# Aggregation of a graph convolution by seven products of 2x2 blocks, with the sums of counts made during the projection

## The chip, the cores and the metric

The kernel runs on one core of a Trainium2 chip. The metric is the device time of one execution in microseconds, as the median of several runs. One further execution was taken with the hardware profiler, and its record is what "the profile" and "the trace" mean here. The engines are TensorE (PE; its weight loads are listed apart as PEld), VectorE (DVE), ScalarE (ACT), GpSimd (POOL) and SyncE (SP). SP only issues DMA transfers; POOL issues some as well.

## The reference

There are 1250 nodes with 1024 features, and 20000 edges. Four parts follow each other, each on a normalized copy of x and added to x: graph attention, a feed-forward layer with a wide projection, a graph convolution, and a layer of eight experts. The change is in the convolution:

```python
x = x + _L0_gnn_ref(_layernorm(x), W, a_l, a_r, src, dst)
x = x + _L0_ffn_ref(_layernorm(x)[None], rail_maker, rail_up_proj, w_cproj)[0]
x = x + _L1_gnn_ref(_layernorm(x), edge_index, W, b)
x = x + _L1_ffn_ref(_layernorm(x)[None], w1s, w2s, w3s, W1, W2, W3, Wg)[0]

def _L1_gnn_ref(x, edge_index, W, b):
    ei = jnp.concatenate([edge_index, jnp.stack([self_idx, self_idx])], axis=1)
    row, col = ei
    h = jnp.einsum('nd,od->no', x, W) + b
    deg = jnp.zeros((num_nodes,)).at[row].add(1.0)
    norm = deg[row] ** -0.5 * deg[col] ** -0.5
    return jax.ops.segment_sum(norm[:, None] * h[col], row, num_segments=num_nodes)
```

Written with matrices, the last line is D (C + I) D h: C counts the edges from each node to each other node, I stands for the edge of each node to itself, and D is the diagonal of deg to the power -0.5.

## The kernel before

The 1250 nodes are ten tiles of 125 (`R` = 125, `T` = 10). While it works on the attention, the kernel builds the counts from the edge list and keeps them in DRAM as `cnt_d[s, p, d, j]`: the number of edges from node j of tile s to node p of tile d. A block of 125x125 counts read this way has the summed index on the partitions, as a matmul's weights need it.

The feed-forward layer comes next and is the longest stage. Its projection multiplies hidden rows with `w_cproj` in 16 blocks. Each block is done as 2x2 blocks by seven products, twice nested: 49 steps in the blocks 0 to 14, and 28 steps in block 15. A step is `product` (four matmuls with 313 columns, L594; the trace has two records for each fp32 matmul), and then `accumulate`: ACT copies the result out of PSUM to one of five buffers `parts` (L603), and a DMA from POOL's queue adds it onto `acc_d` in DRAM (L605 for block 0, L607 for the rest). The sums of blocks of weights and of hidden rows, which the seven products take as factors, are made on DVE by `add_up` (L587) some steps ahead of their use; `projection_plan` lists the steps and decides ahead of which one each sum stands. Hidden rows lie in buffers `YS` of 128 x 626 numbers, which are views into the tiles `X` and `low`. The free ones are the list `yh`, taken by `place_y`, and given back by `used` after their last reader. SP loads the weights (L406, `load_weights`) and the rails of the next block (`load_rails`, L413 and L414). The loop over the steps (L703) holds the order in which all this is issued; in it `b` is the block and `m` the step in the block. A scheduler places the instructions on each engine by this order, and an engine runs its own in order.

In the last block, `x` and the accumulated sums are read back, and `linear` (L779) then computes h for each tile of nodes: DVE adds the bias (L786), and ACT multiplies the rows with `dis`, the diagonal D. The result is `Hs`, ten tiles of 125 x 1024, which takes the memory of `low`.

The aggregation (L847 to L866) goes over the ten row tiles r. For each it has the counts of that row in one of three slots of the tile `first_w`, loaded by `load_counts` three rows ahead (SP's queue; POOL adds the identity to the diagonal block, L795). It makes 20 matmuls: ten column tiles c, two halves g of 512 features, into a PSUM tile `ph` of two banks. DVE multiplies the result with `dis` and adds it into X (L861), normalizes the row (`normalize`, L138 to L145), and SP stores it to `xn_d`. PE turns row r-1 between two rows (`turn`, L153: eight transposes and two copies by ACT), and at r = 5, r = 9 and the end makes the `logits` (L840) that choose the experts. `dma` issues two transfers, for partitions 0 to 111 and 112 to 124 (L105, L106). The layer of experts follows (L885 and after).

The factors of the seven products are the same tables for the projection and for the changed aggregation:

```python
SUMS = {"X": {"s1": ("21", "+", "22"), "s2": ("s1", "-", "11"), "s3": ("11", "-", "21"), "s4": ("12", "-", "s2")},
        "Y": {"s1": ("12", "-", "11"), "s2": ("22", "-", "s1"), "s3": ("22", "-", "12"), "s4": ("s2", "-", "21")}}
FACTORS = {1: ("11", "11"), 2: ("12", "21"), 3: ("s4", "22"), 4: ("22", "s4"), 5: ("s1", "s1"), 6: ("s2", "s2"),
           7: ("s3", "s3")}
```

Of the kernel before, what the change touches and what calls it, by code (L numbers as in the profile page):

```python
# [8 lines left out]
F32 = mybir.dt.float32  # L9
# [5 lines left out]
ALU = mybir.AluOpType  # L15
# [4 lines left out]
P = 128  # L20
R, T = 125, 10
N = R * T
# [12 lines left out]
NS = NE * ROWS // P  # L35
NP = N + 2
NQ = NP // 4
NB = 16


# [2 lines left out]
FACTORS = {1: ("11", "11"), 2: ("12", "21"), 3: ("s4", "22"), 4: ("22", "s4"), 5: ("s1", "s1"), 6: ("s2", "s2"),  # L43
           7: ("s3", "s3")}
# [53 lines left out]
def gnn_ffn_kernel(ctx, tc, x, src, dst, gat_w, a_l, a_r, maker, up, cproj,  # L98
                   gcn_w, gcn_b, w1s, w2s, w3s, w1, w2, w3, wg, out):
    nc = tc.nc  # L100
    ctx.enter_context(nc.allow_non_contiguous_dma(reason="weights by blocks"))

    def dma(eng, out, in_):

        eng.dma_start(out[:RA], in_[:RA])  # L105
        eng.dma_start(out[RA:], in_[RA:])  # L106
# [7 lines left out]
    nm_d = dram.tile([T, R, N], F32, name="nm_d")  # L114
    x_d = dram.tile([T, R, D], F32, name="x_d")

    acc_d = dram.tile([7, 7, P, 2, NQ], F32, name="acc_d")
    xn_d = dram.tile([N, D], F32, name="xn_d")
    tok_d = dram.tile([NE * ROWS + N, 1], I32, name="tok_d")
# [27 lines left out]
    def turn(xT, norm, psp, t, bufs=2, at=None, wide=False):  # L147

        at = t * R if at is None else at
        for g in range(2):  # L150
            pt = psp.tile([P, 4, 512], F32, name="pz2")[:, :, :R] if wide else psp.tile([P, 4, R], F32, name="pt", bufs=bufs)
            for k in range(4):
                nc.tensor.transpose(pt[:, k, :], norm[t][:, (4 * g + k) * P:(4 * g + k + 1) * P], ident[:R, :R])  # L153
            nc.scalar.copy(xT[:, 4 * g:4 * g + 4, at:at + R], pt)
# [229 lines left out]
    X = XX[:R]  # L384
    for t in range(T):
        dma(nc.gpsimd, X[:, t, :], x_t[t])
    HN = N // 2
    HT = T // 2
    norm = {}
    tt = nc.vector.tensor_tensor  # L390

# [146 lines left out]
    with ExitStack() as tail:  # L538
# [26 lines left out]
        def place_y(top):  # L565

            return yh.pop(yh.index(max(yh)) if top else 0)
# [41 lines left out]
        def late_tile(t):  # L609
            xn = scratch[:R, (4 + t % 2 * 2) * 512:][:, :D]  # L610
            normalize(norm, rlp, t, xn)
            turn(xT, norm, zps, t, 1, t * R + 1, wide=True)


        def free_acc(v):
            (yh if v < 32 else early).append(v)
# [81 lines left out]
        last, j = None, 0  # L698
        loads_at = dict(zip((end + v for v in (-13, -6, 1, 7, 12, 15, 20)), OUTER))
        bring = [(end + v, k, outer_sums(w)) for v, k, w in zip((-9, 0, 3, 10, 14, 18, 22), (2, 2, 2, 4, 4, 3, 3), OUTER)]  # L700
        added, sent = [], []
        norm = {}
        for n, (b, p, i, pairs) in enumerate(steps):  # L703
            m = n - 49 * b
            if n >= end - 70:

                xw[:] = [v for v in xw if v < 33]
            for w in (b, b + 1):
                while coming.get(w) and len(xw) > (0 if w == b else 16 if m < 12 else 8 if m < 20 else 4):
                    load_weights(w, *coming[w].pop(0))  # L710
            if b == 0:
                for v in first.get(m, ()):
                    hidden(0, *v)
            while j < len(sums) and sums[j][0] <= n:
                add_up(*sums[j][1:])
                j += 1
            if b == 0 and m in late:
                late_tile(late[m])
                if late[m] == T - 1:
                    xw += range(33, 41)  # L720
            if b == 0 and m == 30:

                for e in range(NE):
                    nc.gpsimd.dma_start(
                        ys_d[:NE * ROWS, :].rearrange("(p s) (a b) -> p s a b", s=NS, b=128)[CAP - P:, 2 * e + 1],
                        zero[CAP - P:].to_broadcast([ROWS - CAP, D // 128, 128]))
            if b + 1 < NB:
                if m == 20:
                    for k in range(2):
                        load_rails(b + 1, k)  # L730
                if m in (28, 30):
                    rails(m // 2 - 14, zps.tile([P, 4, 512], F32, name="pz2")[:, 0, :P])
                if m in later:
                    hidden(b + 1, *later[m])
            assert n != end - 13 or all(v < 33 for k, v in buf.items() if k[1] == "X")
            if n in loads_at:
                load_sums(loads_at[n])
            if n == end:
                blocks.close()
                tl = rest.enter_context(tc.tile_pool(name="tl", bufs=2))  # L740
                psp = rest.enter_context(tc.tile_pool(name="tps3", bufs=2, space=PSUM))
                yh += parts
            if b == NB - 1:
                if m >= 14 and len(W3) < 2 * KD:
                    for g, k in [(g, k) for g in range(2) for k in range(KD)]:
                        with tc.issue_after(sent[0]):
                            at = [v for v in xw if not 8 <= v < 16]
                            if at and (k, g) not in W3:
                                xw.remove(at[0])
                                W3[k, g] = XS[at[0]].rearrange("p q o -> p (q o)")  # L750
                                nc.gpsimd.dma_start(W3[k, g], gcn_w[k * P:(k + 1) * P, g * 512:(g + 1) * 512])
                if m == 23:
                    nc.gpsimd.dma_start(bias, gcn_b.partition_broadcast(R))
                while m >= 16 and len(fetched) < 4 and fetch(len(fetched)):
                    pass
                if m == 22:
                    add_out(0)
                    level(0)
                if m == 24:
                    turn_tile(0)  # L760
                if m == 27:
                    add_out(1)
                    level(1)
            po = product(pairs)
            if last:
                (combine if last[0] == NB - 1 else accumulate)(*last[last[0] == NB - 1:])
            for n0, k, sums_of in bring:
                if n0 <= n:
                    with tc.issue_after(added[-1]) if n > end else nullcontext():
                        for _ in range(k):  # L770
                            next(sums_of, None)
            last = b, p, i, po
# [13 lines left out]
            tt(Hs[:, t, :], ph.rearrange("p a b -> p (a b)"), bias, op=ALU.add)  # L786
            nc.scalar.activation(Hs[:, t, :], Hs[:, t, :], AF.Copy, scale=dis[:, t:t + 1])

        def counts(r):

            return first_w[:R, r % 3 * N:r % 3 * N + N].rearrange("p (t j) -> p t j", j=R)

        def load_counts(r):
            dma(nc.sync, counts(r), cnt_d[r])
            nc.gpsimd.tensor_tensor(counts(r)[:, r, :], counts(r)[:, r, :], ident[:R, :R], op=ALU.add)  # L795

        for t in range(T):
            if 5 <= t < 8:
                load_counts(t - 5)
            for w in range(len(fetched), min(T, t + 5)):  # L800
                fetch(w)
            linear(t)
# [22 lines left out]
        weights(wsh, w1s, w2s, w3s)  # L825
        wgt = keep.tile([P, KD, NE], F32, name="wgt")
        nc.sync.dma_start(wgt, wg.rearrange("(k p) e -> p k e", p=P))
        hs = keep.tile([P, 2, N], F32, name="hs")
        late = keep.tile([R, T, NE], F32, name="late")
        place = keep.tile([R, T], I32, name="place")  # L830
        back = keep.tile([R, T], I32, name="back")
# [4 lines left out]
        def logits(t0, n):  # L836

            pg = psp.tile([NE, 512], F32, name="pg", bufs=1)
            for k in range(KD):
                nc.tensor.matmul(pg[:, :n * R], wgt[:, k, :], xT5[:, k, t0 * R:(t0 + n) * R],  # L840
                                 start=(k == 0), stop=(k == KD - 1))
            lgT = lnp.tile([NE, 512], F32, name="lgT", bufs=2)
            nc.scalar.copy(lgT[:, :n * R], pg[:, :n * R])
            for i in range(n):
                nc.tensor.transpose(pl[:, t0 + i, :], lgT[:, i * R:(i + 1) * R], ident[:NE, :NE])

        for r in range(T):  # L847
            cs = counts(r)
            pa = psp.tile([R, 2, 512], F32, name="ph")
            for c in range(T):  # L850
                for g in range(2):
                    nc.tensor.matmul(pa[:, g, :], cs[:, c, :], Hs[:, c, g * 512:(g + 1) * 512],  # L852
                                     start=(c == 0), stop=(c == T - 1))
            if r:
                turn(xT5, norm, psp, r - 1)
                if r in (5, 9):
                    logits(r - 5, 4)
            if r + 3 < T:
                load_counts(r + 3)
            xs = X[:, r, :]  # L860
            nc.vector.scalar_tensor_tensor(xs, pa.rearrange("p a b -> p (a b)"), dis[:, r:r + 1], xs,  # L861
                                           op0=ALU.mult, op1=ALU.add)
            normalize(norm, lnp, r)
            dma(nc.sync, xn_d[r * R:(r + 1) * R, :], norm[r])
        turn(xT5, norm, psp, T - 1)
        logits(8, 2)  # L866
        lg = lnp.tile([R, T, NE], F32, name="lg", bufs=1)
        nc.vector.tensor_copy(lg, pl)

# [2 lines left out]


    with back_end:
        with tc.tile_pool(name="ab", bufs=2, space=PSUM) as abp, tc.tile_pool(name="tps", bufs=2, space=PSUM) as tps, \
                tc.tile_pool(name="ops6", bufs=1, space=PSUM) as ops:

# [206 lines left out]
```

## Time and profile before

| | us |
|---|---|
| median of 3 runs | 2962.14 (2961.96 to 2962.9) |
| the profiled execution | 2961.7 |
| its span, first to last instruction | 2959.9 |
| PE busy | 2896.8 (98% of the span) |
| DVE busy | 1593.2 (54%) |
| ACT busy | 875.9 (30%) |
| POOL busy | 764.1 (26%) |
| attention and hidden rows, until | 680 |
| projection, blocks 0 to 14, until | 2317 |
| last block and `linear`, until | 2467 |
| aggregation, until | 2668 |
| experts, until | 2959.9 |

The span is what the profiler recorded; the time of the execution has 1.8 us more around it. A busy share is the time in which an engine has an instruction under way. PE can be busy in the record while its matmuls, which overlap, advance slower or faster, so lengths of stages are read from the starts of instructions. An engine that is not on the chain of waits can be far from full without any loss, and can be delayed without any loss until somebody waits for it.

### The profile page before, as it was taken

The page shows a single profiled execution, that of the slowest core. Times are in us where ns is not written, and L with a number is a line of the kernel's source. Part 1 is how long each engine was busy: PE and PEld are TensorE (multiplying, and loading weights), DVE is VectorE, ACT ScalarE, POOL GpSimd, SP SyncE. Part 2 cuts the span into 40 slices and gives each one's busy share as a digit, 9 for nine tenths or more (in the row PEclk, how much of TensorE's full clock was granted, in tenths as well). Part 3 has the DMA queues.
Part 4 walks back from the last instruction along what each step waited for, and adds up shares of the span by engine and source line. Part 5 has one row for each costly group of instructions (what it writes and reads, how often), then busy time and mean ns, then how long its engine had stood idle before and what let it go on. Part 6 is the DMA issues. An engine that isn't in the chain of part 4 may idle for free.

```text
span 2959.9 us, 32455 instructions
## 1 busy us (share of the span) xinstructions
PE 2896.8 (98%) x11479; PEld 1911.6 (65%) x11479; DVE 1593.2 (54%) x2611; ACT 875.9 (30%) x1415; POOL 764.1 (26%) x982
## 2 busy tenths in 40 slices
PE   8999899999999999999999999999999999999997
PEld 5574677666766766766766766766767544445774
DVE  7687887845645645645645645645467431221113
ACT  1221234444344344344344344344330110000000
POOL 2010000224434434434434434434330000002001
PEclk9999999999999999999999999999999999999999
DMA  5245523569999999999999999999994302222655
GB/s 142 65 114 143 152 70 119 186 162 178 194 168 179 195 167 179 194 168 180 192 168 182 191 167 182 192 164 163 208 245 132 81 0 74 62 70 72 215 196 165
DMA packets 252549, 449.58 MB, mean 152 GB/s; under 512 B 48160, under 2 KB 132218, under 8 KB 251753
## 3 DMA queue, kind: packets, MB, share of 16 engines
q0 software_dynamic: 115216, 270.53, 53.7%
q1 hardware_dynamic: 137162, 176.86, 20.3%
q8 instruction: 96, 1.57, 0.2%
q14 instruction: 75, 0.61, 0.1%
HBM read 175.38 MB, written 271.89 MB: 151 GB/s over the span
## 4 chain that ended last, share of the span: by engine, by line
PE 83%; DVE 1%; DMA 1%; ACT 0%; issue 0%; POOL 0%; DVEq 0%; ACTq 0%
PE po L594 56%; PE ph L852 6%; PE pab L885 6%; PE po L779 5%; PE pz L428 3%; PE po L448 3%; PE po L991 2%; PE po L1002 1%; PE pt L153 1%; DMA low<-acc_d 1%; PE pg L840 1%; DMA yg<-ys_d,back 0%; DMA rowbd<-st 0%; PE px L679 0%; PE pt L981 0%
## 5 line engine op out<-in xcount | busy, mean ns | idle before, releaser
L607 POOL DMA_DIRECT2D acc_d<-low x686 | 592.9, 865 | 915.2 <-ACT low L603 890.3
L603 ACT COPY low<-po 128x626 f32<-128x626 f32 x735 | 501.0, 682 | 994.3 <-PE po L594 822.4
L594 PE MATMUL po<-X,arena 128*128 128x313 f32 x2160 | 608.2, 428 | 0.0
L594 PEld LDWEIGHTS po<-X,arena 128*128 128x128 f32 x2160 | 404.8, 189 | 171.3 <-issue 19.2
L594 PE MATMUL po<-low,arena 128*128 128x313 f32 x1568 | 443.5, 428 | 0.0
L594 PEld LDWEIGHTS po<-low,arena 128*128 128x128 f32 x1568 | 294.0, 189 | 123.2 <-issue 12.4
L594 PE MATMUL po<-X,first_w 128*128 128x313 f32 x856 | 243.3, 428 | 0.2 <-DVE first_w L587 0.2
L594 PE MATMUL po<-X,BZ 128*128 128x313 f32 x720 | 207.1, 431 | 0.0
L594 PEld LDWEIGHTS po<-X,first_w 128*128 128x128 f32 x856 | 160.5, 189 | 68.0 <-issue 7.5
L852 PE MATMUL ph<-low,first_w 125*125 125x512 f32 x400 | 173.6, 593 | 1.4 <-issue 1.4
L594 PEld LDWEIGHTS po<-X,BZ 128*128 128x128 f32 x720 | 135.7, 191 | 57.8 <-issue 7.7
L587 DVE TENSOR_TENSOR X<-X 128x626 f32<-128x626 f32 x141 | 114.3, 813 | 101.3 <-PE po L594 99.8
L594 PE MATMUL po<-low,first_w 128*128 128x313 f32 x544 | 155.3, 429 | 0.0
L209 PE MATMUL pz<-W,xT 128*125 128x512 f32 x320 | 141.2, 596 | 0.1
L594 PE MATMUL po<-low,BZ 128*128 128x313 f32 x480 | 138.4, 428 | 0.0
L852 PEld LDWEIGHTS ph<-low,first_w 125*125 125x125 f32 x400 | 74.3, 188 | 94.8 <-issue 94.8
L594 PEld LDWEIGHTS po<-low,first_w 128*128 128x128 f32 x544 | 101.6, 190 | 43.2 <-issue 5.5
L587 DVE TENSOR_TENSOR X<-low,X 128x626 f32<-128x626 f32 x101 | 82.0, 816 | 84.4 <-PE po L594 82.4
L587 DVE TENSOR_TENSOR low<-X 128x626 f32<-128x626 f32 x102 | 82.8, 815 | 69.3 <-PE po L594 69.1
L587 DVE TENSOR_TENSOR X<-X,low 128x626 f32<-128x626 f32 x92 | 75.1, 818 | 80.3 <-PE po L594 80.1
L277 PE MATMUL pc<-os,od 125*125 125x417 f16 (+1 forms) x588 | 110.9, 345 | 5.1 <-issue 5.1
L448 PE MATMUL po<-BZ,w 125*125 125x257 f32 x400 | 96.6, 401 | 19.5 <-DVE w L446 18.2
(263 smaller groups left out, 3405.5 us busy)
## 6 DMA issues: line engine op xcount, KB each, us to landing
acc_d<-low POOLq DMA_DIRECT2D x735, 313.0 KB, 5.9
arena<-in_cproj SPq DMA_DIRECT2D x148, 256.0 KB
w<-in_w SPq DMA_DIRECT2D x16, 1024.0 KB
BZ<-in_cproj SPq DMA_DIRECT2D x56, 256.0 KB
first_w<-in_cproj SPq DMA_DIRECT2D x52, 256.0 KB
nm<-nm_d SPq DMA_DIRECT2D x20, 546.9 KB
w3t<-in_w SPq DMA_DIRECT2D x8, 1024.0 KB
X<-acc_d SPq DMA_DIRECT2D x20, 313.0 KB
```

Of the source, the lines that this page charges most:

```text
L209: nc.tensor.matmul(pz, xT[:, k, t * R:(t + 1) * R], W[g][:, k], start=(k == 0), stop=(k == KD - 1))
L277: nc.tensor.matmul(pc[:, b, :nn], od[:, d - near[c][0], :], os[:, n0:n0 + nn], start=(c == win[d][0]), stop=(c == win[d][-1]))
L428: nc.tensor.matmul(pz, [*rail_parts(k)][-1][rows, :], xT[rows, (2 * b + k) % KD, n * NQ:(n + 1) * NQ], start=True, stop=True)
L448: nc.tensor.matmul(po[i], w[:, i * R:(i + 1) * R], Z[h // 2][:, s, h % 2, :], start=(s == 0), stop=(s == T - 1))
L587: tt(view(k), *a, op=ALU.add if sign == "+" else ALU.subtract)
L594: nc.tensor.matmul(po[:, o, :NQ], view(x)[:, q, o * P:(o + 1) * P], view(y)[:, q, :], start=(i == q == 0), stop=(i + 1 == len(pairs) and q ...
L603: nc.scalar.copy(part, po[:, :, :NQ])
L607: sent[:] = [nc.gpsimd.dma_start(out=acc_d[p - 1, i - 1], in_=part, accum_op=ALU.add).ins]
L779: nc.tensor.matmul(ph[:, g, :], turned[t][:, k, :], W3[k, g], start=(k == 0), stop=(k == KD - 1))
L852: nc.tensor.matmul(pa[:, g, :], cs[:, c, :], Hs[:, c, g * 512:(g + 1) * 512], start=(c == 0), stop=(c == T - 1))
L885: nc.tensor.matmul(pab[:, :nn], w12[:, i, k, f * P:(f + 1) * P], rhs[:, k, n0:n0 + nn], start=(k == 0), stop=(k == KD - 1))
L991: nc.tensor.matmul(po[:m, g, :], hid[:, f, s * P:s * P + m], w3t[:, f, g * 512:(g + 1) * 512], start=(f == 0), stop=(f == 1))
```

## The change

The aggregation is written as a product of 2x2 blocks, (C + I) by `Hs`. A block of C + I is 5 x 5 tiles of 125; a block of `Hs` is five tiles by 512 features. Seven products with sums of blocks take the place of eight products of blocks.

The sums of counts are made within the projection. In each of the blocks 2 to 6, at step 24, `load_pair` takes four `YS` buffers and loads into them one column tile c and its partner c + 5 of the counts (eight transfers on SP, with runs of 125 numbers, 500 bytes). At step 31 `sum_pair` adds the identity to the two diagonal blocks, makes the four sums s1 to s4 on DVE, stores them to `s_d` in DRAM (eight transfers on SP), and gives the buffers back.

The aggregation is then a list of 35 items (p, a): product p, row tile a of five. An item is five matmuls of 512 columns into one PSUM bank, with four banks in rotation. Its counts, half as wide as before, lie in one of six slots and are loaded six items ahead, from `s_d` or from `cnt_d`. Each result is added on DVE straight into the halves of rows of X which it belongs to (`into`: one to four of them; a new tile `ndis` has the negative of `dis`). The sums of `Hs` are made on DVE, up to three after each item; s1 and s2 have a new tile each, s3 overwrites block 12, and s4 block 21 once product 2 is done. A row is complete with product 3 or 4, and is normalized then; it is turned two items later. The tile `hs` of the experts moves to another pool.

```diff
+    s_d = dram.tile([4, HT, R, HT, R], F32, name="s_d")
...
+        def as_counts(i):
+            return YS[i].rearrange("p q n -> p (q n)")[:R, :HN].rearrange("p (a j) -> p a j", j=R)
+
+        def load_pair(c):
+            pair[:] = [place_y(False) for _ in range(4)]
+            for i, (s0, d) in zip(pair, ((0, c), (HT, c), (0, c + HT), (HT, c + HT))):
+                dma(nc.sync, as_counts(i), cnt_d[s0:s0 + HT, :, d, :].rearrange("s p j -> p s j"))
+
+        def sum_pair(c):
+            x11, x21, x12, x22 = (as_counts(i) for i in pair)
+            for v in (x11, x22):
+                tt(v[:, c, :], v[:, c, :], ident[:R, :R], op=ALU.add)
+            tt(x22, x21, x22, op=ALU.add)
+            tt(x21, x11, x21, op=ALU.subtract)
+            tt(x11, x22, x11, op=ALU.subtract)
+            tt(x12, x12, x11, op=ALU.subtract)
+            for k, v in enumerate((x22, x11, x21, x12)):
+                dma(nc.sync, s_d[k, :, :, c, :].rearrange("a p j -> p a j"), v)
+            yh.extend(pair)
...
+            if 2 <= b < 2 + HT:
+                if m == 24:
+                    load_pair(b - 2)
+                if m == 31:
+                    sum_pair(b - 2)
...
+        work = [(p, a) for p in (1, 2, 6) for a in range(HT)]
+        work += [(p, a) for w in ((5, 3), (7, 4)) for a in range(HT) for p in w]
+
+        def counts(i):
+            return first_w[:R, i % 6 * HN:i % 6 * HN + HN].rearrange("p (c j) -> p c j", j=R)
+
+        def load_counts(i):
+            p, a = work[i]
+            cs = counts(i)
+            f = FACTORS[p][0]
+            if f[0] == "s":
+                dma(nc.sync, cs, s_d[int(f[1]) - 1, a])
+                return
+            d0 = HT * (f[1] == "2")
+            dma(nc.sync, cs, cnt_d[HT * (f[0] == "2") + a][:, d0:d0 + HT, :])
+            if f[0] == f[1]:
+                nc.gpsimd.tensor_tensor(cs[:, a, :], cs[:, a, :], ident[:R, :R], op=ALU.add)
...
-                load_counts(t - 5)
+                load_counts(2 * t - 10)
+                load_counts(2 * t - 9)
...
-        hs = keep.tile([P, 2, N], F32, name="hs")
...
-        for r in range(T):
-            cs = counts(r)
-            pa = psp.tile([R, 2, 512], F32, name="ph")
-            for c in range(T):
-                for g in range(2):
-                    nc.tensor.matmul(pa[:, g, :], cs[:, c, :], Hs[:, c, g * 512:(g + 1) * 512],
-                                     start=(c == 0), stop=(c == T - 1))
-            if r:
-                turn(xT5, norm, psp, r - 1)
-                if r in (5, 9):
-                    logits(r - 5, 4)
-            if r + 3 < T:
-                load_counts(r + 3)
-            xs = X[:, r, :]
-            nc.vector.scalar_tensor_tensor(xs, pa.rearrange("p a b -> p (a b)"), dis[:, r:r + 1], xs,
-                                           op0=ALU.mult, op1=ALU.add)
-            normalize(norm, lnp, r)
-            dma(nc.sync, xn_d[r * R:(r + 1) * R, :], norm[r])
-        turn(xT5, norm, psp, T - 1)
-        logits(8, 2)
+        sp = tail.enter_context(tc.tile_pool(name="tsum", bufs=1))
+        Y = {f"{1 + i}{1 + j}": Hs[:, HT * i:HT * i + HT, j * 512:(j + 1) * 512] for i in range(2) for j in range(2)}
+        Y["s1"], Y["s2"] = (sp.tile([R, HT, 512], F32, name=f"y{i}") for i in range(2))
+        Y["s3"], Y["s4"] = Y["12"], Y["21"]
+
+        def sum_h(k, c):
+            u, sign, v = SUMS["Y"][k]
+            tt(Y[k][:, c], Y[u][:, c], Y[v][:, c], op=ALU.add if sign == "+" else ALU.subtract)
+
+        sums_h = [(k, c) for k in ("s1", "s2", "s3") for c in range(HT)]
+        into = {1: ((0, 0, 1), (0, 1, 1), (1, 0, 1), (1, 1, 1)), 2: ((0, 0, 1),), 3: ((0, 1, 1),), 4: ((1, 0, -1),),
+                5: ((0, 1, 1), (1, 1, 1)), 6: ((0, 1, 1), (1, 0, 1), (1, 1, 1)), 7: ((1, 0, 1), (1, 1, 1))}
...
+        def turn_ready():
+            t = ready.pop(0)[1]
+            turn(xT5, norm, psp, t)
+            if t in (4, 8, 9):
+                logits(*{4: (0, 4), 8: (4, 4), 9: (8, 2)}[t])
+
+        for i, (p, a) in enumerate(work):
+            cs = counts(i)
+            pa = psp.tile([R, 512], F32, name="ph", bufs=4)
+            for c in range(HT):
+                nc.tensor.matmul(pa, cs[:, c, :], Y[FACTORS[p][1]][:, c], start=(c == 0), stop=(c == HT - 1))
+            if i + 6 < len(work):
+                load_counts(i + 6)
+            if ready and ready[0][0] <= i - 2:
+                turn_ready()
+            for h, j, sign in into[p]:
+                r = HT * h + a
+                xs = X[:, r, j * 512:(j + 1) * 512]
+                nc.vector.scalar_tensor_tensor(xs, pa, (dis if sign > 0 else ndis)[:, r:r + 1], xs,
+                                               op0=ALU.mult, op1=ALU.add)
+            if (p, a) == (2, HT - 1):
+                sums_h += [("s4", c) for c in range(HT)]
+            for _ in range(min(3, len(sums_h))):
+                sum_h(*sums_h.pop(0))
+            if p in (3, 4):
+                r = a if p == 3 else HT + a
+                normalize(norm, lnp, r)
+                dma(nc.sync, xn_d[r * R:(r + 1) * R, :], norm[r])
+                ready.append((i, r))
+        while ready:
+            turn_ready()
...
+        hs = back_end.enter_context(tc.tile_pool(name="hsp", bufs=1)).tile([P, 2, N], F32, name="hs")
```

More of the change, by code (lines that the diff above doesn't have):

```diff
@@ L37 @@
 NQ = NP // 4
+HN, HT = N // 2, T // 2
 NB = 16
@@ L386, in gnn_ffn_kernel @@
         dma(nc.gpsimd, X[:, t, :], x_t[t])
-    HN = N // 2
-    HT = T // 2
     norm = {}
@@ L700, in gnn_ffn_kernel @@
         bring = [(end + v, k, outer_sums(w)) for v, k, w in zip((-9, 0, 3, 10, 14, 18, 22), (2, 2, 2, 4, 4, 3, 3), OUTER)]
-        added, sent = [], []
+        added, sent, pair = [], [], []
         norm = {}
@@ L787, in linear @@
             nc.scalar.activation(Hs[:, t, :], Hs[:, t, :], AF.Copy, scale=dis[:, t:t + 1])
[L789 to L795, printed above, removed]
+        work = [(p, a) for p in (1, 2, 6) for a in range(HT)]
[13 more added lines that the diff above has]
+                nc.gpsimd.tensor_tensor(cs[:, a, :], cs[:, a, :], ident[:R, :R], op=ALU.add)
         for t in range(T):
             if 5 <= t < 8:
-                load_counts(t - 5)
+                load_counts(2 * t - 10)
+                load_counts(2 * t - 9)
             for w in range(len(fetched), min(T, t + 5)):
@@ new lines, in gnn_ffn_kernel @@
+        sums_h = [(k, c) for k in ("s1", "s2", "s3") for c in range(HT)]
+        into = {1: ((0, 0, 1), (0, 1, 1), (1, 0, 1), (1, 1, 1)), 2: ((0, 0, 1),), 3: ((0, 1, 1),), 4: ((1, 0, -1),),
+                5: ((0, 1, 1), (1, 1, 1)), 6: ((0, 1, 1), (1, 0, 1), (1, 1, 1)), 7: ((1, 0, 1), (1, 1, 1))}
+        ndis = lnp.tile([R, T], F32, name="ndis", bufs=1)
+        nc.vector.tensor_scalar(ndis, dis, -1.0, None, op0=ALU.mult)
+        ready = []
+        def turn_ready():
[3 more added lines that the diff above has]
+                logits(*{4: (0, 4), 8: (4, 4), 9: (8, 2)}[t])
```

## The prediction

> **What bounds the kernel now.** I read the chain of waits first, then the table of windows by stage, then PE's waits inside the two stages that the diff touches, and last the groups by engine. Part 4 of the page:
>
> ```profile
> PE 83%; DVE 1%; DMA 1%; ACT 0%; issue 0%; POOL 0%; DVEq 0%; ACTq 0%
> PE po L594 56%; PE ph L852 6%; PE pab L885 6%; PE po L779 5%; PE pz L428 3%; PE po L448 3%; PE po L991 2%; PE po L1002 1%; PE pt L153 1%; DMA low<-acc_d 1%; PE pg L840 1%; DMA yg<-ys_d,back 0%; DMA rowbd<-st 0%; PE px L679 0%; PE pt L981 0%
> ```
>
> TensorE sets the end, and the two touched places, the projection (L594) and the aggregation (L852), are both on the chain. The windows of these stages (length, busy time and count of PE, PEld, DVE, ACT, POOL, then clock, DMA share, GB/s):
>
> ```profile
> 680.00:2317.00 1637.00, 1636.82 (x6745) 1127.36 (x6744) 937.64 (x1317) 603.81 (x922) 623.28 (x735) 1.00 1.02 180
> 2467.00:2668.00 201.00, 199.66 (x538) 88.48 (x538) 38.31 (x63) 16.25 (x34) 4.04 (x13) 1.00 0.26 83
> ```
>
> PE is without gaps in both. Other engines have room: DVE is busy 57% of the projection and 19% of the aggregation. Matmul busy times are modelled, so I take pitch from starts in PE's timeline (start, us, ..., count):
>
> ```profile
> 2467.57 34.57 PE L852 MATMUL ph<-low,first_w 125*125 125x512 f32 x80 [1.36 <-issue]
> 2501.98 1.02 PE L153 MATMUL pt<-ident,xn 125*128 125x125 f32 x8
> 2502.83 17.33 PE L852 MATMUL ph<-low,first_w 125*125 125x512 f32 x40
> 2520.00 1.02 PE L153 MATMUL pt<-ident,xn 125*128 125x125 f32 x8
> 2520.86 9.61 PE L852 MATMUL ph<-low,first_w 125*125 125x512 f32 x22
> ```
>
> A row of tiles is 20 matmuls, recorded as 40. Groups of 40 and 22 give a pitch of (17.33 - 9.61)/18 = **0.429 us per record**, and 0.17 us of tail. Starts of two rows lie 18.03 us apart: 40 x 0.429 = 17.16, and 0.87 for eight transposes. Inside the group of 80 lies one change of row without transposes: 34.57 - 80 x 0.429 - 0.17 = 0.08 us, the most that such a boundary costs.
>
> **What the Trainium skill says.** "Perfetto Trace Analysis", section Identifying the Most-Contended Engine: matmul busy share is no measure of roofline, and occupancy of 16 DMA engines misleads. The trace agrees: a DMA share of 1.02 in the projection stands beside this, all that PE waited for there from 680 to 2330 us:
>
> ```profile
> PE po L594 <- DVE first_w L587: 0.2, 1, 0.2
> ```
>
> "VectorE: DVE Perf Modes", section The TRN2 errata: an fp32 tensor_tensor of N elements takes (N + 151)/0.96 ns: 809 at 626 and 691 at 512. The trace has 813 at 626, and 686 to 690 at 512; I use its figures. "DMA: Bandwidth & Descriptors", section Specifications: below 512 bytes a transfer loses line rate. The new pair transfers have packets of 500 bytes. Early in the kernel (110 to 145 us) such packets are seen alone (packets, MB, share of 16 engines):
>
> ```profile
> q1 hardware_dynamic: 2857, 2.49, 28.3%
> ```
>
> That is 28.3% of 35 us, 9.9 us of all engines, for about 2,600 packets of 500 bytes and 1.1 MB more.
>
> **The change, part by part.**
>
> *Matmuls.* The aggregation goes from 200 matmuls (10 rows x 10 column tiles x 2 halves) to 175 (35 products x 5), each still 125x512. Every matmul has its own weight load before (400 PEld beside 400 records) and after. 25 matmuls are 50 records: 50 x 0.429 = **-21.45 us**, on the path. Transposes and logits stay the same in number.
>
> *Boundaries.* 35 products instead of 10 rows, each waiting for a PSUM buffer and a counts slot: 25 more at 0 to 0.08 us. Of the 0.87 us that eight transposes add, 8 x 125/512 x 0.429 = 0.84 is the columns', so 0.03 a boundary is likely: **+0.7** (0 to 2).
>
> *Evictions.* The old one is this:
>
> ```profile
> L861 DVE SCALAR_TENSOR_TENSOR X<-ph,dis,X 125x1024 f32<-125x1024 f32 x10 | 12.8, 1284 | 148.3 <-PE ph L852 148.3
> ```
>
> 1284 ns is 1024 cycles at 0.96 and 209 more, so one of 512 should take (512 + 209)/0.96 = 0.75 us (estimate). There are 70: four per product in p=1, one in p=2, three in p=6, three per pair of (5,3) and of (7,4). Twenty sums of Hs at 0.69 come three per product at first. A product lasts 5 x 2 x 0.429 = 4.29 us. In p=1, DVE has 4 x 0.75 + 3 x 0.69 = 5.07 us per product: it falls 0.8 behind each time, 3.9 us over five, and four PSUM buffers (3 x 4.29 us ahead) cover that; p=2 (0.75 us) pays it back. The pairs with normalization (2.9 us) have 5.1 us for 8.6. DVE's sum is 70 x 0.75 + 20 x 0.69 + 10 x 2.5 = 91 us of 180. **0**; without that cover PE would wait at most 3.9 us.
>
> *Count loads.* SP now issues 70 counts DMAs rather than 20, half as wide, into six slots, each loaded six products (25.7 us) ahead. At the least 35 x 312 KB in 176 us is 62 GB/s, and this stage moves 83 now. The first loads hang on the same last projection steps as before. **0** (0 to +2).
>
> *Sums of counts in blocks 2 to 6.* Each block gets eight more loads (1.25 MB), six DVE operations (four of 625 elements at 0.81, two of 125 at about 0.29: 3.8 us) and eight stores (1.25 MB). In the built order the loads wait for their buffers until steps 16 to 21 of the block, and the last of DVE's waits on them stands at step 24. The first result behind that wait which PE needs is for step 33: the last load may take 12 steps, less some DVE work, about 22 us, while all four take 10 us alone, or 16 us if only (260 - 180) GB/s are left. On SP, weight loads of the next block and the rails' queue behind the stores; their users come most of a block (111 us) later. POOL's queue is not passed through, but shares the DMA engines: **0** taken, with 0 to +1 us per block, 0 to +5 in all. DVE's own waits show where its 3.8 us lie:
>
> ```profile
> DVE X L587 <- PE po L594: 110.5, 60, 6.8
> DVE low L587 <- PE po L594: 82.5, 43, 6.8
> ```
>
> These are 193 us of DVE idling for PE between 900 and 1500 us.
>
> *The end.* The last tile's normalization is hidden now:
>
> ```profile
> 2654.83 6.87 PE L840 MATMUL pg<-xT,wgt 128*8 128x500 f32 x16
> ...
> 2657.49 0.81 DVE L145 TENSOR_SCALAR xn<-X,mv,rstd 125x1024 f32<-125x1024 f32 x1
> ```
>
> DVE ends at 2658.3, the logits at 2661.7. Afterwards the order is again last product, transposes of tile 8, logits of four tiles, transposes of tile 9; one half-width eviction comes last instead of 1.28 us. **0** (-0.2 to +0.5). The new `ndis` is one small operation beside the start. The tile `hs` moves to another pool and is not written earlier. **0**.
>
> *Sum.* -21.45 + 0.7 = -20.75. The profiled execution took 2961.7 us (span 2959.9, 1.8 around it): 2940.95. The median shown lies 0.44 above it: **2941.4**.
>
> **Rivals.**
>
> *A, as summed:* 2941.4, with 2939 to 2943.5 for the unknown terms at their usual sizes. Chance 0.76.
>
> *B, pair traffic stalls the projection, slower.* The place is the accumulation into acc_d. ACT copies a result to one of five buffers, POOL sends it, and the buffer is free on landing:
>
> ```profile
> DMA to landing us min/median/max: 4.7/5.9/8.7
> ```
>
> A step takes 2.1 us (with what lies between, 49 steps are 111), so the ring allows 10.5 us, less 0.68 for ACT and 0.87 for POOL: a landing of 8.95. With the hardware queue busy, landings rise from 5.1 to 7.5 us in the median. If 500-byte packets push them to L us, a step takes (L + 1.55)/5. Over 16 steps (loads and stores) and with 2 us of slack in PSUM, L = 11.3 costs 16 x 0.47 - 2 = 5.5 us per block and 27 in five: this is the point, where 20.75 are used up and 5.9 more are lost, 2968. For it: the maximum is near the limit already. Against: the hardware queue is nearly idle at steps 31 to 46, where the stores go, and other stretches moved 234 GB/s with PE at 100%. Chance 0.04 of slower, 0.04 of about no change (L near 11, 2957 to 2968), and 0.08 of a partial cost (L near 10, 1 to 2 us per block, 2944 to 2952).
>
> *C, DVE sets the pace of the aggregation.* The cover is 12.9 us. With an eviction of 1.4 us in place of 0.75, a product of p=1 costs DVE 4 x 1.4 + 3 x 0.69 = 7.67 us, 3.38 more than PE takes, 16.9 over five: +4 us, 2945. Against: 1284 ns for twice the elements. Chance 0.04.
>
> *D, late counts or an uncovered end:* a DMA wait of 2 us in some products, +3, 2944. Chance 0.04. That the change doesn't do what it says is ruled out as to count: 175 matmuls are built.
>
> **How the numbers follow.** 0.2% (5.9 us) is about what a measurement of this kernel can tell from no change. Faster by more: A, C, D and the partial case of B, 0.92; within it 0.04; slower 0.04. The range, 2938.5 to 2947, takes A with both bounds, C, D and about half of B's partial case, near 0.88, since the bounds of the estimates may be too tight.
>
> **What would show it.** After: 350 records of 125x512 under the aggregation at 0.429 us pitch; stage about 21 us shorter; 70 evictions near 0.75 us; PE still without waits in the projection; blocks 2 to 6 still 111.3 us; landings of acc_d under 8.95. It is wrong if blocks 2 to 6 are longer than block 7 (B), if PE waits for DVE at ph in p=1 or p=6 (C), or for a counts load (D).

## The result, and the profile after

The median is **2941.81 us** (2939.97 to 2943.15, four runs), against 2962.05 for the kernel before in the same series: a ratio of 0.9931, with a 95% interval from 0.9919 to 0.9944. That is 20 us less. The forecast was 2941.4, within 2938.5 to 2947. The profiled execution took 2939.97 us with a span of 2938.3.

The chain of waits of the changed kernel still runs through PE, and the aggregation's share has fallen by a point:

```profile
PE 84%; DVE 1%; DMA 1%; ACT 0%; issue 0%; POOL 0%; DVEq 0%; SPq 0%; ACTq 0%
PE po L594 57%; PE pab L955 6%; PE ph L915 5%; PE po L805 5%; PE pz L428 3%; PE po L448 3%; PE po L1061 2%; PE po L1072 1%; PE pt L155 1%; PE pg L879 1%; DMA rowbd<-st 0%; DMA X<-x_d 0%; PE px L700 0%; DMA yg<-ys_d,back 0%; PE pt L1051 0%
```

The windows of the projection and of the aggregation (length, busy time and count of PE, PEld, DVE, ACT, POOL, clock, DMA share, GB/s):

```profile
680.00:2317.00 1637.00, 1636.87 (x6745) 1127.30 (x6744) 945.72 (x1347) 603.76 (x922) 620.30 (x735) 1.00 1.03 188
2467.00:2646.00 179.00, 178.20 (x488) 79.12 (x488) 87.46 (x144) 16.25 (x34) 3.25 (x11) 1.00 0.39 117
```

The projection has the same length, filled by PE just as before, although DVE has 30 operations more in it and the transfers rise from 180 to 188 GB/s. (The 30 operations last 19 us one by one, as forecast; DVE's busy time rises by only 8, since operations that directly follow each other overlap in the record.) The aggregation has 50 PE records fewer and more than twice the work on DVE (38.3 us before). PE's timeline has its start, and the start of the experts (L955):

```profile
2467.11 43.15 PE L915 MATMUL ph<-low,first_w 125*125 125x512 f32 x100 [1.36 <-issue]
...
2641.39 3.54 PE L879 MATMUL pg<-xT,wgt 128*8 128x250 f32 x16
2645.43 0.38 PE L884 MATMUL pl<-ident,lgT 8*125 8x8 f32 x2 [0.50 <-ACT lgT L882]
2646.15 11.47 PE L955 MATMUL pab<-xT,w12s 128*128 128x417 f32 x32 [0.33 <-DVE lg L937]
```

From the first product to the experts pass 2646.15 - 2467.11 = 179.04 us. Before, they began at 2668.06:

```profile
2668.06 2.37 PE L885 MATMUL pab<-xT,w12s 128*128 128x417 f32 x6 [0.33 <-DVE lg L868]
```

So 2668.06 - 2467.57 = 200.49 us passed. The difference is **21.45 us**, which is 50 x 0.429. The stages ahead of it took 0.46 us less in this execution and the experts 0.3 more, which leaves 21.6 in the span.

### The profile page after: what moved, and what is told of

Its sections match the earlier page's. It is cut to its first block, busy times and chain, and to the rows that moved or that the text cites. A ratio compares the mean times of both kernels' runs of the same rounds, so it can differ in the third digit from the quotient of the medians.

```text
span 2938.3 us, 32714 instructions
## 1 busy us (share of the span) xinstructions
PE 2879.8 (98%) x11429; PEld 1904.0 (65%) x11429; DVE 1651.7 (56%) x2722; ACT 875.7 (30%) x1415; POOL 760.8 (26%) x982
## 4 chain that ended last, share of the span: by engine, by line
PE 84%; DVE 1%; DMA 1%; ACT 0%; issue 0%; POOL 0%; DVEq 0%; SPq 0%; ACTq 0%
PE po L594 57%; PE pab L955 6%; PE ph L915 5%; PE po L805 5%; PE pz L428 3%; PE po L448 3%; PE po L1061 2%; PE po L1072 1%; PE pt L155 1%; PE pg L879 1%; DMA rowbd<-st 0%; DMA X<-x_d 0%; PE px L700 0%; DMA yg<-ys_d,back 0%; PE pt L1051 0%
## 5 line engine op out<-in xcount | busy, mean ns | idle before, releaser
L594 PE MATMUL po<-X,BZ 128*128 128x313 f32 x688 | 196.8, 430 | 0.0
L594 PEld LDWEIGHTS po<-X,BZ 128*128 128x128 f32 x688 | 129.8, 191 | 53.7 <-issue 5.6
L594 PE MATMUL po<-low,BZ 128*128 128x313 f32 x512 | 147.6, 429 | 0.0
L594 PEld LDWEIGHTS po<-low,BZ 128*128 128x128 f32 x512 | 95.6, 189 | 41.5 <-issue 6.0
L915 PE MATMUL ph<-low,first_w 125*125 125x512 f32 x250 | 109.5, 593 | 1.4 <-issue 1.4
L587 DVE TENSOR_TENSOR X<-low,X 128x626 f32<-128x626 f32 x90 | 72.9, 816 | 66.1 <-PE po L594 64.1
L587 DVE TENSOR_TENSOR low<-X 128x626 f32<-128x626 f32 x89 | 73.2, 823 | 60.4 <-PE po L594 59.0
```

Of the source, the lines that this page charges most:

```text
L587: tt(view(k), *a, op=ALU.add if sign == "+" else ALU.subtract)
L594: nc.tensor.matmul(po[:, o, :NQ], view(x)[:, q, o * P:(o + 1) * P], view(y)[:, q, :], start=(i == q == 0), stop=(i + 1 == len(pairs) and q ...
L915: nc.tensor.matmul(pa, cs[:, c, :], Y[FACTORS[p][1]][:, c], start=(c == 0), stop=(c == HT - 1))
```

## The experiments

All ratios are to the kernel before on the same chip. The experiments ran in three series. The changed kernel was run again in the first of them only and is the reference for all; the kernel before has medians of 2961.69, 2961.6 and 2961.26 in the three, so they lie within half a microsecond of each other. The expectation for the reference:

> The changed kernel itself, beside the experiments of this group on one chip. Every theory: about 20 us under the kernel before (2941 to 2943 against 2962). It serves as the reference for the other three.

Measured: 2942.03 us (2937.84 to 2945.14, five runs), ratio 0.9936 [0.9922, 0.9949].

**The work in the projection left out.** Its diff:

```diff
-            if 2 <= b < 2 + HT:
-                if m == 24:
-                    load_pair(b - 2)
-                if m == 31:
-                    sum_pair(b - 2)
...
-                dma(nc.sync, cs, s_d[int(f[1]) - 1, a])
+                dma(nc.sync, cs, cnt_d[a][:, :HT, :])
```

> Leaves out the loads, sums and stores of counts in blocks 2 to 6; the aggregation reads plain counts in place of their sums. Theory A (the work is hidden behind PE): the same as the changed kernel within 1 us, and landings of the accumulations at steps 31 to 37 of blocks 2 to 6 fall from 10-11 us to 5-6. Theory B (the pair traffic costs the projection something): 1 to 5 us faster than the changed kernel.

Measured: 2941.06 us (2936.72 to 2944.95), ratio 0.9932 [0.9918, 0.9946], 1 us from the reference and inside its spread. The starts of the first accumulations of blocks 2 and 7 lie 556.8 us apart in both kernels, and in the kernel before too. So the loads, sums and stores cost nothing that can be measured. They do leave a mark. Landings of the accumulations in these five blocks (748 to 1305 us; a landing is the time from the start of POOL's instruction until the data has arrived), first of the changed kernel:

```profile
DMA to landing us min/median/max: 4.7/6.9/11.1
```

and without the work on the counts:

```profile
DMA to landing us min/median/max: 4.6/5.9/8.6
```

The second trace has only 153 of the 245 landings, but the kernel before, with all of them, has nearly the same (4.7/5.9/8.7).

**Only the saving undone.** Eight products of blocks in the new structure:

```diff
-        work = [(p, a) for p in (1, 2, 6) for a in range(HT)]
-        work += [(p, a) for w in ((5, 3), (7, 4)) for a in range(HT) for p in w]
+        EIGHT = {1: ("11", "11"), 2: ("12", "21"), 3: ("11", "12"), 4: ("12", "22"), 5: ("21", "11"), 6: ("22", "21"),
+                 7: ("21", "12"), 8: ("22", "22")}
+        work = [(p, a) for p in (1, 2) for a in range(HT)]
+        work += [(p, a) for w in ((3, 4), (5, 6, 7, 8)) for a in range(HT) for p in w]
...
-        sums_h = [(k, c) for k in ("s1", "s2", "s3") for c in range(HT)]
+        sums_h = []
+        into = {p: ((p > 4, p in (3, 4, 7, 8), 1),) for p in EIGHT}
...
-            if p in (3, 4):
-                r = a if p == 3 else HT + a
+            if p in (4, 8):
+                r = a if p == 4 else HT + a
...
```

> Only the saving of matmuls is undone: eight products of blocks (200 matmuls, 40 results added into X, no sums of Hs) in the new structure, with the pair work of the projection left in though nothing reads it. Theory A (25 matmuls are the whole gain): 21.4 us slower than the changed kernel and level with the kernel before, within 1.5 us. Rival (part of the gain is from the structure: single banks, narrow evictions, a shorter end): faster than the kernel before by over 2 us.

Measured: 2968.35 us (2966.18 to 2972.85, 11 runs), ratio 1.0027 [1.0018, 1.0036]: 26 us over the reference, 5 more than expected, and a miss for both readings. PE's timeline shows where they are:

```profile
2469.58 60.32 PE L916 MATMUL ph<-low,first_w 125*125 125x512 f32 x140 [1.36 <-issue]
...
2656.63 7.99 PE L916 MATMUL ph<-low,first_w 125*125 125x512 f32 x18
2667.91 1.05 PE L155 MATMUL pt<-ident,xn 125*128 125x125 f32 x8 [3.28 <-DVE xn L147]
2669.19 5.23 PE L881 MATMUL pg<-xT,wgt 128*8 128x250 f32 x16 [0.24 <-ACT xT L156]
...
2675.63 11.47 PE L954 MATMUL pab<-xT,w12s 128*128 128x417 f32 x32 [0.33 <-DVE lg L936]
```

In this order tile 8 is ready four items ahead of the last product, so its transposes and logits had already been done. Nothing was left to lie beside the normalization of tile 9, and PE waited 3.28 us for it; the logits behind it took 5.23 us in place of 3.54; why they did is left open. From the first product to the experts it takes 2675.63 - 2469.58 = 206.05 us, 5.56 more than in the kernel before.

**The same with rows turned later.**

```diff
-            if ready and ready[0][0] <= i - 2:
+            if ready and ready[0][0] <= i - 4:
```

> As the eight products before, but a row is turned four items after its completion instead of two, so that the transposes of tile 8 and the logits of four tiles come behind the last product again and the last normalization lies beside them. Theory A (25 matmuls are the whole gain; the extra of the first try was the uncovered end): 21.4 us slower than the changed kernel, level with the kernel before within 1.5 us. Rival (the structure itself costs 5 us, and the seven products gain 26): stays near 2968.

Measured: 2961.26 us (2958.77 to 2966.48, 13 runs), ratio 1.0001 [0.9993, 1.001]: level with the kernel before. From the first product to the experts (L954) it takes 2667.71 - 2467.22 = 200.49 us, the kernel before's figure:

```profile
2467.22 68.90 PE L916 MATMUL ph<-low,first_w 125*125 125x512 f32 x160 [1.36 <-issue]
...
2667.71 11.47 PE L954 MATMUL pab<-xT,w12s 128*128 128x417 f32 x32 [0.34 <-DVE lg L936]
```

Two things follow. The 25 matmuls are the whole gain of the stage, and 40 items take as long as ten rows, so a boundary costs nothing that shows. And one line of order at the end is worth 206.05 - 200.49 = 5.56 us in the stage, and 7 us between the medians of the two series.

**Two PSUM buffers in place of four.**

```diff
-            pa = psp.tile([R, 512], F32, name="ph", bufs=4)
+            pa = psp.tile([R, 512], F32, name="ph", bufs=2)
```

> Two PSUM buffers for the results in place of four, everything else as in the changed kernel. If DVE's backlog in product 1 is real (0.8 us per item) and the buffers hide it: PE waits for DVE at ph from the fifth item on, about 0.3, 0.8 and 0.8 us, 2 us in all, none later; time +2. If DVE keeps up without the buffers: no wait of PE at ph, time unchanged. If DVE is much nearer to its limit than estimated: waits in product 6 and in the pairs too, over 5 us.

Measured: 2941.13 us (2937.9 to 2945.66), ratio 0.9932 [0.9917, 0.9947], and PE waits for no eviction (an eviction is DVE's reading of a result out of PSUM). DVE's timeline in this kernel says why (start, us, then count):

```profile
2470.31 3.18 DVE L894 TENSOR_TENSOR y<-low 125x512 f32<-125x512 f32 x5
2473.41 1.88 DVE L894 TENSOR_TENSOR y<-low,y 125x512 f32<-125x512 f32 x3
2475.22 2.71 DVE L923 SCALAR_TENSOR_TENSOR X<-ph,dis,X 125x512 f32<-125x512 f32 x4
2477.86 1.28 DVE L894 TENSOR_TENSOR y<-low,y 125x512 f32<-125x512 f32 x2
2479.09 2.73 DVE L923 SCALAR_TENSOR_TENSOR X<-ph,dis,X 125x512 f32<-125x512 f32 x4
2481.74 1.89 DVE L894 TENSOR_TENSOR low<-low 125x512 f32<-125x512 f32 x3
2483.54 2.72 DVE L923 SCALAR_TENSOR_TENSOR X<-ph,dis,X 125x512 f32<-125x512 f32 x4
2486.18 1.28 DVE L894 TENSOR_TENSOR low<-low 125x512 f32<-125x512 f32 x2
2487.68 2.73 DVE L923 SCALAR_TENSOR_TENSOR X<-ph,dis,X 125x512 f32<-125x512 f32 x4 [0.22 <-PE ph L915]
```

Eight of the sums were placed ahead of the first eviction, nearly all of them while PE was still at the first item (2470.24 to 2474.5). With each of the next three items go two or three sums. An item with four evictions and three sums takes DVE 2483.54 - 2479.09 = 4.45 us, where the prediction had 5.07, and PE needs 4.29. At the fourth item DVE waits for PE again (0.22 us): the backlog that the buffers were thought to cover hardly arises.

**Stores in wide runs.** The sums go to DRAM with 2500 bytes per partition; the loads of the aggregation gather the 500-byte runs instead.

```diff
-                dma(nc.sync, s_d[k, :, :, c, :].rearrange("a p j -> p a j"), v)
+                dma(nc.sync, s_d[k, c], v)
...
-                dma(nc.sync, cs, s_d[int(f[1]) - 1, a])
+                dma(nc.sync, cs, s_d[int(f[1]) - 1, :, :, a, :].rearrange("c p j -> p c j"))
```

> The sums are stored with runs of 2500 bytes per partition; the 500-byte runs move to the 20 loads of the sums in the aggregation. If the narrow packets of the stores make the landings of 10-11 us: they fall to 7-8 us at steps 31 to 37 of blocks 2 to 6. If the volume does (1.25 MB beside the accumulations): they stay near 10. Time in both cases that of the changed kernel within 1 us, since PE waits for neither; unless the narrow loads are late in the aggregation (up to +3).

Measured: 2940.93 us (2940.0 to 2941.9), ratio 0.9931 [0.9917, 0.9945]. The longest landing in blocks 2 to 6 is 9.5 us instead of 11.1, between the two expectations, but this decides nothing: the trace has only 122 of the 245 landings there, and the kernels with narrow stores and the same work in the projection reach 10.8 (eight products), 10.6 (rows turned later) and 9.8 (two buffers). That the volume counts is shown by the run without the work; what the width adds to the landings is not. DVE's wait for stores that still read a buffer is shorter with wide runs. In the changed kernel, from 740 to 1310 us (us in total, times, longest):

```profile
DVE X L587 <- DMA s_d<-X: 39.0, 6, 9.8
```

and with wide stores:

```profile
DVE X L587 <- DMA s_d<-X: 5.8, 3, 3.1
```

This wait varies from run to run, but the direction holds: the reference had 18.4 us there, and the three kernels just named 16.4 to 19.2.

**Every sum stored twice.**

```diff
+    s2_d = dram.tile([4, HT, R, HT, R], F32, name="s2_d")
...
                 dma(nc.sync, s_d[k, :, :, c, :].rearrange("a p j -> p a j"), v)
+                dma(nc.sync, s2_d[k, :, :, c, :].rearrange("a p j -> p a j"), v)
```

> Every sum of counts is stored twice, the second time to a tensor that nothing reads: 2.5 MB in 500-byte runs per block. Theory A (the ring has room: at steps 31 to 46 every second step is followed by hidden rows of the next block, a step takes 2.6 us on average there, and five buffers allow landings of 5 x 2.6 - 1.55 = 11.5 us): the stretch of late landings gets longer, PE waits for nothing, blocks 2 to 6 stay 111.3 us. Rival B (the ring is at its limit): landings past 11.5, PE waits at po, blocks 2 to 6 longer by 1 to 5 us each.

Measured: 2955.57 us (2946.56 to 2972.23, 12 runs), ratio 0.9988 [0.9977, 1.0]: 13.5 us over the reference, most of the gain. Neither theory had it right. The longest landing is 11.1 us as with single stores, and PE never waits at `po`. PE waits at `pz`, the PSUM tile in which hidden rows of the next block are made, until ACT has read it:

```profile
PE pz L429 <- ACT X L581: 3.8, 3, 2.2
```

ACT writes those hidden rows into buffers of `YS`, and among them are the four that `sum_pair` has given back while the stores still read them. ACT's waits in the same stretch, and its timeline at one of them:

```profile
ACT X L581 <- DMA s_d<-X: 15.3, 4, 5.1
ACT low L581 <- DMA s_d<-low: 3.6, 1, 3.6
...
1283.37 0.69 ACT L581 ACTIVATE low<-pz 128x626 f32<-128x626 f32 x1
1289.18 0.69 ACT L581 ACTIVATE X<-pz 128x626 f32<-128x626 f32 x1 [5.12 <-DMA s_d<-X]
1289.77 1.26 ACT L604 COPY low<-po 128x626 f32<-128x626 f32 x2
```

While ACT stands there, the copies out of PSUM queue behind it (two at once at 1289.77). The profiled execution is the shortest of the 12, with blocks 2 to 6 longer by 4.8 us, of which PE's waits at `pz` make 4.5. The longer runs have no profile, so that the rest of the 13.5 us has the same cause is argued from this one and from the next experiment.

**Stored twice, buffers given back later.** Against the kernel of the last experiment:

```diff
-            yh.extend(pair)
...
                 if m == 31:
                     sum_pair(b - 2)
+                if m == 44:
+                    yh.extend(pair)
```

> Sums stored twice in 500-byte runs as before, but the four buffers go back to the list of free ones at step 44 instead of 31, so that hidden rows and sums written from step 32 to 44 no longer wait for the stores to have read them. Theory W (the 14 us of the doubled stores are writes into buffers that are still being stored, and ACT standing in that wait with PE's accumulator behind it): back to 2942 within 3 us, no wait of ACT for s_d. Theory R (the DMA traffic itself delays the accumulations and the weight loads): stays above 2950.

Measured: 2942.19 us (2941.19 to 2945.38), ratio 0.9935 [0.9918, 0.9952]. The doubled traffic is the same and the cost is gone, so theory W holds: it was the reuse of the buffers while they were being stored, and the doubled traffic alone costs nothing that shows. The two traces also tell on which engine the wait matters. ACT waits for no store any more; DVE still does, 80 us in these blocks as against 73.5 with the buffers given back at step 31, and the time does not suffer. This kernel has the longest landing of all, and one wait of ACT for the ring, that is, for one of the five buffers `parts` to be free again:

```profile
DVE low L588 <- DMA s_d<-low: 42.6, 5, 18.7
DVE X L588 <- DMA s_d<-X: 37.3, 3, 16.1
...
ACT low L604 <- DMA acc_d<-low: 2.0, 1, 2.0
...
DMA to landing us min/median/max: 5.1/7.4/11.9
```

**Stored twice in wide runs.** The diff is that of the wide stores with a second store of the same form.

> Sums stored twice with runs of 2500 bytes, buffers given back at step 31. If the narrow packets make the stores slow: these doubled stores end as early as the single narrow ones or earlier, time within 3 us of the changed kernel (2942), ACT's waits for s_d gone or under 1 us. If bytes count and not packets: as with the doubled narrow stores, near 2955.

Measured: 2940.64 us (2939.68 to 2949.05, four runs), ratio 0.9927 [0.991, 0.9943]. The median is that of the changed kernel, so packets count and not bytes alone. The margin is not large. The profiled execution is the one of 2949, and in it DVE stood 61 us for stores in blocks 2 to 6, ACT once 3.6 us, and these blocks took 2 us longer. About half of its excess of 8 us lies elsewhere: PE waited 4.3 us for a sum of weights at 2161 us, long after the last of these stores.

**Four buffers in place of five on the way to acc_d.**

```diff
-        yh, parts, early = [*range(4, 8), *range(16, 27), *range(8, 16)], list(range(27, 32)), list(range(32, 38))
+        yh, parts, early = [*range(4, 8), *range(16, 27), *range(8, 16)], list(range(28, 32)), list(range(32, 38))
...
```

> Four buffers for the results on their way to acc_d in place of five. The ring then allows 4 x 2.6 - 1.55 = 8.9 us at steps 31 to 46 and 4 x 2.1 - 1.55 = 6.9 us at other steps. If the ring is what sets the limit: PE waits at po in blocks 2 to 6 at steps 31 to 37, where landings are near 10 (up to 1 us per block beyond the slack of PSUM), and some at steps 5 to 16 of all blocks (landings 7.7); together 0 to 10 us slower. If landings shorten when fewer are under way: no wait, time unchanged.

Measured: 2943.95 us (2942.17 to 2950.15), ratio 0.9946 [0.9931, 0.9961], not to be told from the reference. Blocks 2 to 6 are 1 us longer in all. ACT does meet the ring now (740 to 1310 us; us of idle time that a landing ended, times, longest), which with five buffers it never did in the changed kernel:

```profile
ACT low L603 <- DMA acc_d<-low: 110.8, 71, 3.5
```

Much of this idle time is what ACT otherwise spends waiting for PE, and PE waits at `po` for none of it in these blocks. So even when the ring holds ACT up, the time barely changes.

## Why the prediction was right, by its own steps

*Matmuls, -21.45:* right, shown from both sides: the stage shrank by 21.45 us, and grew back to 200.49 us with the 25 matmuls put back.

*Boundaries, +0.7:* too much. 0 in the trace, with 35 items and with 40. Beside the matmuls it is the only term of the sum with a size, and it was wrong by 0.7 us, below what the medians can tell.

*Evictions, 0:* the price was right, the story around it was not. The half-width eviction, by groups of DVE in the changed kernel:

```profile
L923 DVE SCALAR_TENSOR_TENSOR X<-ph,dis,X 125x512 f32<-125x512 f32 x65 | 45.6, 745 | 65.2 <-PE ph L915 65.2
```

745 ns against an estimate of 750, and DVE's busy time in the stage came to 87.5 us against 91. But the 3.9 us of backlog assumed three sums behind the evictions of every item, as the code is written; the scheduler put eight ahead. And it added up operations at their single length, where four evictions in a row take 2.71 us, so they start (2.71 - 0.745)/3 = 0.66 us apart. The Trainium skill's "VectorE: DVE Perf Modes", section The TRN2 errata, gives 120 + N cycles at 0.96 GHz for a PSUM source, by which 512 columns take 658 ns (an estimate): the trace agrees with it as spacing, not as the duration of one. Rival C was further away than it was priced.

*Count loads, 0:* right; PE waited for none.

*Work on the counts, 0:* the size was right and is shown by leaving it out; two reasons given for it were not. First, the limit of 8.95 us on landings was passed (11.1) without a stall. It used the block's shortest step, 2.1 us, but at steps 31 to 46 about every second step is followed by hidden rows, and the starts of the accumulations in the trace are 2.1 or 3.05 us apart, 2.55 on average. It also took off POOL's 0.87 us, which lies inside a landing as it is counted. The closest case of this trace is in block 6: the result copied from 1260.47 was sent at 1261.45 and landed 11.1 us later, at 1272.5, and the fifth copy after it, which takes the same buffer, began at 1272.90 (engine ACT, then POOL):

```profile
1260.47 0.68 ACT L603 COPY low<-po 128x626 f32<-128x626 f32 x1 [1.43 <-PE po L594]
...
1272.90 0.68 ACT L603 COPY low<-po 128x626 f32<-128x626 f32 x1 [1.43 <-PE po L594]
...
1261.45 0.86 POOL L607 DMA_DIRECT2D acc_d<-low  x1 [1.26 <-ACT low L603]
```

The room was 1272.90 - 1261.45 = 11.45 us, and 0.4 of it was left. So the ring was nearer to its limit than a projection without waits suggests; the experiment with four buffers adds that 71 waits of ACT for the ring lengthened these blocks by 1 us. Second, rival B looked for its stall in that ring. The experiments with doubled stores put it at the same stores but in another wait, one that the prediction named for no step: a buffer given back at step 31 is still being read by its store when ACT or DVE next writes it. With single stores only DVE meets it, and has the time. Doubled, ACT meets it too, and 13.5 of 20 us go.

*DVE behind the loads, 22 us of room:* consistent. DVE waited 71 us for pair loads in the five blocks, 11.9 at the longest, and PE for none of it.

*The end, 0:* right, and the order was what kept it so: the first try with eight products lost that cover and paid 5.56 us in the stage.

*The sum:* that it came within 0.4 us of the median is in part luck. The runs spread over 3.2 us, and without the mistaken 0.7 the sum would lie 1.1 us below the median. The stage gained 21.45 us, the medians 20.2 in this series and 19.7 in the next; the difference is inside the spread and was not traced.

## What to carry to other kernels

Where the trace shows an engine on the chain without gaps through a stage, fewer instructions on it are worth their pitch, as they were here, and the rest of the forecast is a list of covers: name what hides each new piece and what comes due when it no longer does. A buffer that is given back after the instruction that issues its store is not yet free; ask who writes it next, and on which engine that wait will stand: here 80 us of such waits on DVE cost nothing, and 19 us on ACT made the blocks 4.8 us longer. Take the room of a ring from the stretch where it is used, not from the shortest step.

## What the runs showed of the hardware

Stores of 1.25 MB that SP issues lengthened the landings of the accumulating transfers that POOL issues beside them. From 1256 to 1276 us the landings of the changed kernel are 7.4, 9.7 and 11.1 us (shortest, median, longest), those of the kernel before 4.7, 5.6 and 6.6, and PE ran on without gaps in both.

Stores in wider runs held up the next users of their buffers less: DVE's waits for them in blocks 2 to 6 come to between 16 and 40 us in five profiles with 500-byte runs, and to 5.8 in one with 2500-byte runs. With every sum stored twice, the time is 2955.57 us with the narrow runs and 2940.64 with the wide ones. The Trainium skill ("DMA: Bandwidth & Descriptors", Specifications) asks for transfers of at least 512 bytes for the full rate. The runs agree in direction; none shows where the line lies.

Operations of DVE that directly follow each other take less together than one by one: four evictions 2.71 us, where one takes 0.745.
